# A decoder layer with routed experts: the lists of expert blocks in fewer VectorE operations

## The chip, the cores and the metric

The kernel runs on one core of one Trainium2 chip. The metric is the device time of one execution in microseconds (us); the time of a kernel is the median of its runs. TensorE is called PE here, VectorE DVE, ScalarE ACT, GpSimd POOL and SyncE SP, as in the profile.

## The reference

One decoder layer in float32, for 8 sequences of 112 tokens (896 rows of 512). Three sublayers, each followed by a sum with its input and a layernorm:

```python
x = _layernorm(x + attn(x, W_Q, W_K, W_V, W_O))              # 16 heads of 128, causal softmax
x = _layernorm(x + xattn(x, ctx_2048, Wq, Wg, bg, Wkv, Wo))  # linear attention over 375 rows, gated
x = _layernorm(x + ffn(x, router, gate_up, down))            # 8 experts of 512, two per token
```

The last one is what the change touches:

```python
logits = h @ router_weight.T + router_bias
top_vals, top_idx = jax.lax.top_k(logits, TOP_K)             # TOP_K = 2 of E = 8
top_w = jax.nn.softmax(top_vals, axis=-1)
scores = jnp.zeros_like(logits).at[jnp.arange(T)[:, None], top_idx].set(top_w)
gate_up = jnp.einsum('th,ehj->etj', h, gate_up_proj) + gate_up_proj_bias[:, None, :]
...
act = (up + 1.0) * (gate * jax.nn.sigmoid(gate * ALPHA))     # gate and up clipped at 7
expert_out = jnp.einsum('eti,eih->eth', act, down_proj) + down_proj_bias[:, None, :]
out = jnp.einsum('te,eth->th', scores, expert_out)
```

The kernel computes an expert only for the tokens routed to it.

## The kernel before, in words

**Stages.** The 896 rows are 7 tiles of 128. Self-attention runs first, head by head. Then cross-attention: for each sequence b the projections of its context (`project_pair`, matmuls L776), a summary of keys and values (`summarize`, L830), and the division and gating (`attend`, L858 to L870: a reciprocal L868 and the product L870 into `gate`). As soon as the rows of tile t are gated, the generator `close(t)` runs beside this work in small pieces, one piece at each `tick()`: the output projection (L261) and the sum (L268), the second layernorm (statistics L239 and L241 on DVE, square root L243 on ACT, L245 and L246 on DVE), and then the router `route(t)`.

**Router.** `route(t)` transposes the rows (L530, copied by ACT at L533), multiplies them with the router's weights (L537), picks the two best experts (L545 to L554), and counts with two matmuls (L562, L563) how many rows each expert has had. `upto[:, t, e]` starts at e * 896 (T is 896) and grows by tile: it is the next free row of expert e in a store in DRAM, where each expert owns 7 blocks of 128 rows. L587 scatters the rows there (two indirect DMAs from POOL).

**Lists.** The expert phase runs in 18 steps. Each handles 128 rows of one expert, or, in the 8 "paired" steps, twice 64 rows of one or two experts. Which expert and which block a step takes is not known until the router has counted, so `list_blocks(i)` computes it on DVE, at five points: after tiles 3, 4 and 5 for the steps 0, 1 to 2 and 3 to 4 (lists 0 to 2, only full blocks), and after the last tile for the last five steps (list 3) and the paired ones (list 4, in blocks of 64 rows). All of it is on tiny tiles: 8 experts, 1 to 8 steps, the same on every partition. For each list the kernel takes the count of an expert's rows, compares it with the block limits `blocks7` (L633) and sums the results (L618): the number of blocks. What earlier lists had (`taken`) is subtracted (`left`, L641), a running sum over experts follows (L646), which is compared with the step's own number in `place` (L650, `past`). The sum of `past` is the step's expert (`es`, as integer `eb[:, 0]`), and the sum of `past` times `jump` (L652 to L654) is the step's block (`eb[:, 1]`, L662). L682 to L686 work out how many blocks each expert got, for the next list. For the last list `changed` (L669) notes whether a step's expert differs from that of the step before in the same buffer, so that its weights need no new load.

**Who reads the lists.** SP reads `eb` into registers (L921) and issues the loads of the expert's weights (L952 `wg` and `wu`, L962 `wd`, 1 MB each, into `slab`), ACT does so for the biases (L987), POOL for the blocks of tokens (L1006). `start(s)` compares a token's first expert with `es` (L1054).

**Order.** The order of the instructions on PE, DVE, ACT and SP is the order in which the program issues them. It is fixed from the start of the loop over b. In this order a list stands on DVE just behind `route(t)` of its tile and ahead of what the loop does next: behind list 0 come the sum and the layernorm of tile 4; behind list 1 the key maps (L788 to L806) and the gating (L867 to L870); behind list 2 the spreading of step 0's biases (L995); behind lists 3 and 4 the spreading of step 2's biases, the sum of step 0's result (L1183), and the gate and up values of step 2 (L1151 to L1160), which PE transposes next (L1040, `aT_ps`). Each engine works its queue in that order, each instruction waiting for its own inputs.

**Expert steps.** In a step PE multiplies with `wg` and `wu` (L1143, `gups`), DVE adds the biases and makes the gated product, PE transposes it and multiplies with `wd` (L1172, `yps`). Twelve slabs hold the weights of four lanes; a lane's next weights are fetched when PE has read the old ones. Steps 5 to 12 are the paired ones; the fetch of step 5 is the first that needs list 4.

Of the kernel before, what the change touches and what calls it, by code (L numbers as in the profile page):

```python
# [10 lines left out]
F32 = mybir.dt.float32  # L11
# [3 lines left out]
ALU = mybir.AluOpType  # L15
AX = mybir.AxisListType
# [3 lines left out]
P = 128  # L20
B, S, D = 8, 112, 512
T = B * S
NT = T // P
# [6 lines left out]
E, I = 8, 512  # L30
W = 516
XF, XD, XS, XK = 512, 513, 514, 515
NB = T // P
NQ = 4
HB = P // 2
# [25 lines left out]
def decoder_layer(ctx: ExitStack, tc: tile.TileContext, t_in: dict, out: bass.AP):  # L61
    nc = tc.nc

    const = ctx.enter_context(tc.tile_pool(name="const", bufs=1))
# [38 lines left out]
    def counting(name: str, shape, pattern):  # L103
        c = const.tile(shape, F32, name=name)
        nc.gpsimd.iota(
            c,
            pattern=pattern,
            base=0,
            channel_multiplier=0,
            allow_small_or_imprecise_dtypes=True,  # L110
        )
        return c
# [5 lines left out]
        out=before,  # L118
# [7 lines left out]
    allones = const.tile([P, P], F32, name="allones")  # L126
    nc.vector.memset(allones, 1.0)
    expert = counting("expert", [P, E], [[1, E]])
    blocks7 = counting("blocks7", [P, E, NB], [[0, E], [P, NB]])

    place = []
    for i, (_, at) in enumerate(LISTS[:-1]):
        n = at.stop - at.start
# [20 lines left out]
    upto = counting("upto", [P, NT + 1, E], [[0, NT + 1], [T, E]])  # L154
# [443 lines left out]
    es = const.tile([P, STEPS], F32, name="es")  # L598
    eb = const.tile([P, 3, STEPS], I32, name="eb")

    taken = const.tile([P, len(LISTS) + 1, E + 1], F32, name="taken")
    nc.vector.memset(taken, 0.0)

    totals = {}

    def list_blocks(i: int):

        t, steps = LISTS[i]
        n = steps.stop - steps.start
# [7 lines left out]
        def summed(out, e_last):  # L617
            nc.vector.tensor_reduce(out, e_last, AX.X, ALU.add)  # L618
            return out

        def per_step(e_row):
            return e_row.unsqueeze(1).broadcast_to([P, n, E])

        left, upto_e, jump = each("left"), each("upto_e"), each("jump")
        if not last:
            count = each("count")
            nc.vector.tensor_sub(count, upto[:, t, :], upto[:, 0, :])  # L627
            several = (False, True) if t == NT else (True,)
            for over_half in several:
                cmp = const.tile([P, E, NB], F32, name=f"cmp_{i}_{over_half}")  # L630
                if t == NT and over_half:
                    nc.vector.tensor_scalar_add(count, count, -float(HB))
                nc.vector.tensor_tensor(  # L633
                    cmp,
                    count.unsqueeze(2).broadcast_to([P, E, NB]),
                    blocks7,
                    ALU.is_gt if t == NT else ALU.is_ge,
                )

                totals[over_half] = summed(each(f"total{over_half}"), cmp if t == NT else cmp[:, :, 1:])  # L640
            nc.vector.tensor_sub(left, totals[True], had[:, :E])  # L641
        else:
            nc.vector.tensor_scalar_mul(had, had, 2.0)
            nc.vector.tensor_add(left, totals[False], totals[True])
            nc.vector.tensor_sub(left, left, had[:, :E])
        nc.vector.tensor_tensor_scan(  # L646
            upto_e, allones[:, :E], left, 0.0, ALU.mult, ALU.add
        )
        past = const.tile([P, n, E], F32, name=f"past_{i}")
        nc.vector.tensor_tensor(past, per_step(upto_e), place[i], ALU.is_le)  # L650

        nc.vector.tensor_sub(jump, had[:, 1:], had[:, :E])  # L652
        nc.vector.tensor_sub(jump, jump, left)
        nc.vector.tensor_scalar_add(jump, jump, float(of_expert))  # L654
        summed(es[:, steps], past)
        nc.vector.tensor_scalar_min(es[:, steps], es[:, steps], float(E - 1))
        nc.vector.tensor_copy(eb[:, 0, steps], es[:, steps])
        nc.vector.tensor_mul(past, past, per_step(jump))
        blk = const.tile([P, n], F32, name=f"blk_{i}")
        summed(blk, past)  # L660
        nc.vector.tensor_add(blk, blk, place[i][:, :, 0])
        nc.vector.tensor_scalar(  # L662
            eb[:, 1, steps], blk, had[:, 0:1], float(E * of_expert), ALU.add, ALU.min
        )

        def changed(now, then, half=None):
            on = slice(0, P) if half is None else slice(half * HB, (half + 1) * HB)
            a, b = es[on, now], es[on, then]
            nc.vector.tensor_tensor(  # L669
                eb[on, 2, now], a, b.broadcast_to(a.shape), ALU.not_equal  # L670
            )
# [31 lines left out]
    with tc.tile_pool(name="cross", bufs=2) as cr:  # L703
# [213 lines left out]
        halves = store.rearrange("(n p) w -> n p w", p=HB)  # L917
# [168 lines left out]
        for b in range(B):  # L1086
# [6 lines left out]
            else:  # L1093
                work = iter(())
                steps = [start(0, side, "bT")]
# [24 lines left out]
    with tc.tile_pool(name="moe", bufs=2, reuse_waits="tile") as moe:  # L1120
# [182 lines left out]
        for s in range(STEPS + 1):  # L1303
# [53 lines left out]
            if before_:  # L1357
# [75 lines left out]
```

## Time and profile before

| what | value |
|---|---|
| time before | 978.79 us, median of 3 runs (977.5, 978.79, 979.02) |
| the profiled execution | 978.09 us, of which the span is 976.5 |
| PE busy | 920.5 us, 94% of the span, 3915 matmuls |
| DVE busy | 502.6 us, 51%, 1117 instructions |
| ACT busy, POOL busy | 247.3 us, 206.1 us |
| mean granted clock of PE | 0.98 |
| lists 0, 1, 2 on DVE | 675.77 to 679.48, 701.42 to 705.19, 736.49 to 740.29 |
| lists 3 and 4 on DVE | 759.65 to 767.74 |

The profile is one execution seen by the hardware profiler. Times count from the start of the span. A row of the timeline gives start, duration, engine, line, operation and output<-input; brackets at its end give the time that the engine was idle before it and what ended that. A row of waits gives the engine, the line that waited, the engine and line that released it, and then total, number and longest of the waits in us. In the view of stretches, each engine's busy us and instructions stand for a stretch of time, then the granted clock of PE (1.00 is full), the mean busy share of the DMA engines, and GB/s.

Lists 0 to 2 are 21 DVE instructions each, lists 3 and 4 together 39. Each takes 0.15 to 0.4 us, and many overlap with the one before.

### The profile page before, as it was taken

Reading aid. Unit: us, or ns where it says so; the run is one execution under the profiler, and the core shown is the slowest. Engines: PE = TensorE matmul, PEld = TensorE weight load, DVE = VectorE, ACT = ScalarE, POOL = GpSimd, SP = SyncE. Lnnn points to the kernel's source line nnn. Section 1 sums busy time; section 2 is a strip of 40 time slices with the busy share of each in tenths; the row PEclk is TensorE's granted clock in tenths of the full one; section 3 lists DMA queues with packets and bytes.
Section 4 is the critical chain, followed back from the end, with each engine's and each line's share of the span. In section 5 each row is a group of like instructions: output and inputs, shape, how many; then the busy total and the mean of one; then the engine's idle time right before and its main releaser. Section 6 shows DMA issues by size and latency. Waiting matters only on the chain. (4 is left out here: it accounts for less than half of the span.)

```text
span 976.5 us, 11044 instructions
## 1 busy us (share of the span) xinstructions
PE 920.5 (94%) x3915; PEld 467.9 (48%) x3915; DVE 502.6 (51%) x1117; ACT 247.3 (25%) x429; POOL 206.1 (21%) x267
## 2 busy tenths in 40 slices
PE   7998999999999999999999999997969999999981
PEld 3465644466445564664554445454544443334440
DVE  1356521145312552456430756677558864556785
ACT  1133311033102330332322233322224322222232
POOL 3133300021101230302002212212102332222343
PEclk9999999999999999999999999999979999999997
DMA  8995004102011001021100111112356899768953
GB/s 339 348 349 210 1 1 172 44 0 87 1 44 43 1 1 43 1 89 60 32 1 1 32 33 54 54 55 69 143 212 258 282 366 371 270 240 342 386 180 133
DMA packets 35063, 130.48 MB, mean 134 GB/s; under 512 B 3862, under 2 KB 8022, under 8 KB 25152
## 3 DMA queue, kind: packets, MB, share of 16 engines
q1 hardware_dynamic: 29296, 114.01, 32.0%
q0 software_dynamic: 4768, 14.98, 4.3%
q10 hardware_dynamic: 944, 0.79, 0.3%
q8 instruction: 31, 0.51, 0.2%
q14 instruction: 24, 0.20, 0.1%
HBM read 122.02 MB, written 30.06 MB: 156 GB/s over the span
## 5 line engine op out<-in xcount | busy, mean ns | idle before, releaser
L1143 PE MATMUL gups<-slab,bT 128*64 128x512 f32 (+1 forms) x416 | 134.1, 602 | 1.2 <-DMA slab<-in_wu_dram 1.2
L261 PE MATMUL ops<-slab,zT 128*128 128x512 f32 x224 | 97.9, 593 | 0.0
L1143 PEld LDWEIGHTS gups<-slab,bT 128*64 128x64 f32 (+1 forms) x416 | 49.1, 160 | 69.5 <-issue 67.4
L299 POOL TENSOR_TENSOR ws<-slab 128x256 f32<-128x256 f32 x16 | 11.6, 727 | 281.1 <-PE qk_5c L315 83.0
L1172 PE MATMUL yps<-slab,aT 128*64 128x512 f32 (+1 forms) x208 | 68.2, 601 | 0.9 <-ACT aT L1044 0.7
L261 PEld LDWEIGHTS ops<-slab,zT 128*128 128x128 f32 x224 | 42.0, 190 | 50.3 <-issue 49.5
L351 PE MATMUL vps<-slab,x0T 128*112 128x512 f32 x128 | 59.4, 619 | 1.0 <-DVE x0T L211 0.8
L1151 DVE TENSOR_TENSOR gu<-gups,biases 128x512 f32<-128x512 f32 x36 | 24.8, 689 | 59.5 <-PE gups L1143 59.5
L268 DVE TENSOR_TENSOR xn<-xn,ops 128x512 f32<-128x512 f32 x28 | 19.2, 685 | 55.3 <-PE ops L261 55.2
L1044 ACT COPY aT<-aT_ps 128x512 f32<-128x512 f32 x18 | 10.5, 585 | 133.5 <-PE aT_ps L1040 133.4
L1172 PEld LDWEIGHTS yps<-slab,aT 128*64 128x64 f32 (+1 forms) x208 | 24.8, 160 | 37.7 <-issue 35.2
L466 DVE COPY zT<-zps 128x448 f32<-128x448 f32 x32 | 20.0, 624 | 39.8 <-PE zps L459 39.8
L459 PEld LDWEIGHTS zps<-pT,v 112*128 112x128 f32 x256 | 33.5, 192 | 12.3 <-issue 11.2
L351 PEld LDWEIGHTS vps<-slab,x0T 128*112 128x112 f32 x128 | 23.0, 185 | 31.7 <-issue 30.0
L435 DVE TENSOR_REDUCE nm<-p 112x4 f32<-112x448 f32 x32 | 19.7, 615 | 30.5 <-POOL p L425 30.5
L261 PE MATMUL xops<-slab,gate 128*128 128x512 f32 x56 | 27.4, 635 | 7.1 <-DVE gate L870 7.1
L459 PE MATMUL zps<-pT,v 112*128 112x112 f32 x256 | 33.4, 273 | 0.0
L587 POOL DMA_INDIRECT store<-xn,rows x14 | 14.0, 1000 | 82.5 <-DVE count L627 58.8
L1185 POOL DMA_INDIRECT parts<-y,nums x16 | 16.9, 1056 | 62.6 <-DVE y L1183 48.6
L995 DVE STREAM_SHUFFLE biases<-biases 128x1024 f32<-128x1024 f32 (+1 forms) x28 | 30.0, 1104 | 0.0
L419 ACT ACTIVATE p<-sps 112x448 f32<-112x448 f32 x32 | 17.4, 543 | 45.6 <-PE sps L411 45.6
L411 PE MATMUL sps<-k,q 128*112 128x112 f32 x256 | 28.0, 262 | 0.0
(816 smaller groups left out, 1676.6 us busy)
## 6 DMA issues: line engine op xcount, KB each, us to landing
slab<-in_wg_dram SPq DMA_DIRECT2D x26, 1024.0 KB
slab<-in_wu_dram SPq DMA_DIRECT2D x26, 1024.0 KB
slab<-in_wd_dram SPq DMA_DIRECT2D x26, 1024.0 KB
store<-slab SPq DMA_DIRECT2D x8, 1806.0 KB
cT<-in_ctxT_dram SPq DMA_DIRECT2D x8, 750.0 KB
slab<-in_wq_dram SPq DMA_DIRECT2D x4, 1024.0 KB
slab<-in_wk_dram SPq DMA_DIRECT2D x4, 1024.0 KB
slab<-in_wo_dram SPq DMA_DIRECT2D x4, 1024.0 KB
```

The costliest lines, as they stand in the source:

```text
L261: nc.tensor.matmul(ps, aT[:, c, t * P : (t + 1) * P], w[:, c, :], start=(c == 0), stop=(c == C - 1),)
L268: nc.vector.tensor_add(xn[:, t, :], xn[:, t, :], ps)
L351: nc.tensor.matmul(ps[:S, :], xT[:, c, b * S : (b + 1) * S], w[:, c, :], start=(c == 0), stop=(c == C - 1),)
L411: nc.tensor.matmul(ps[:S, i * S : (i + 1) * S], qk["q"][:, rows], qk["k"][:, rows], start=True, stop=True,)
L419: nc.scalar.activation(p.rearrange("s b m -> s (b m)"), ps[:S, :HALF], AF.Copy, scale=1.0 / math.sqrt(DH),)
L435: nc.vector.tensor_reduce(nm, p, AX.X, ALU.max, negate=True)
L459: nc.tensor.matmul(zps[:, i * S : (i + 1) * S], v[:, half * 4 + i, hl * DH : (hl + 1) * DH], pT[:, i * S : (i + 1) * S], start=True, stop= ...
L466: nc.vector.tensor_copy(zT[:, hl, half * HALF : (half + 1) * HALF], zps[:, :HALF])
L995: nc.vector.stream_shuffle(b, b, [0] * XH)
L1143: nc.tensor.matmul(ps[rows_], st["bT"][:, c, rows_], slab[3 * q + k][:, c, :], start=(c == 0), stop=(c == C - 1),)
L1151: nc.vector.tensor_add(a, ps, st["bias"][:, k * I : (k + 1) * I])
L1172: nc.tensor.matmul(ps[rows_], st["aT"][:, c, rows_], slab[3 * q + 2][:, c, :], start=(c == 0), stop=(c == C - 1 and s < STEPS - 1),)
```

## The change

`list_blocks` computes the same lists with fewer operations, and three constants or tiles change with it. On DVE a list of the first three has 13 instructions instead of 21, and the last two together have 24 instead of 39. The order on PE, ACT, POOL and SP stays.

- The constant `blocks7` (8 x 7) becomes `first_rows` (8 x 14): for each expert the first rows of its half blocks, e * 896 + 64 k. `upto` is compared with it directly, so the count is no longer worked out; full blocks are every second entry. With all tiles in, one comparison with all 14 gives both sums: of the odd entries for list 3, of all for list 4.
- `jump` is made in one operation, for 7 experts instead of 8, from `taken` and the total. `past` has 7 experts too, so that the expert's number can't pass 7 and the clamp goes.
- The product of `past` and `jump` is written into `place`, whose eighth entry still holds the step's number: the sum over it gives the block without another addition.
- The running sum is written behind a zero (`ends_`), so that it can be read shifted by one. What each expert got comes from it in two operations instead of five. The zeros need five small memsets at the start.

```diff
-    blocks7 = counting("blocks7", [P, E, NB], [[0, E], [P, NB]])
+    first_rows = counting("first_rows", [P, E, 2 * NB], [[T, E], [HB, 2 * NB]])
...
+    jumps = [const.tile([P, E], F32, name=f"jump_{i}") for i in range(len(LISTS))]
+    ends_ = [const.tile([P, E + 1], F32, name=f"ends_{i}") for i in range(len(LISTS))]
+    for x in ends_:
+        nc.vector.memset(x[:, 0:1], 0.0)
...
-            count = each("count")
-            nc.vector.tensor_sub(count, upto[:, t, :], upto[:, 0, :])
-            several = (False, True) if t == NT else (True,)
-            for over_half in several:
-                cmp = const.tile([P, E, NB], F32, name=f"cmp_{i}_{over_half}")
-                if t == NT and over_half:
-                    nc.vector.tensor_scalar_add(count, count, -float(HB))
-                nc.vector.tensor_tensor(
-                    cmp,
-                    count.unsqueeze(2).broadcast_to([P, E, NB]),
-                    blocks7,
-                    ALU.is_gt if t == NT else ALU.is_ge,
-                )
-                totals[over_half] = summed(each(f"total{over_half}"), cmp if t == NT else cmp[:, :, 1:])
-            nc.vector.tensor_sub(left, totals[True], had[:, :E])
+            begun = first_rows if t == NT else first_rows[:, :, 2::2]
+            cmp = const.tile([P, *begun.shape[1:]], F32, name=f"cmp_{i}")
+            nc.vector.tensor_tensor(
+                cmp,
+                upto[:, t, :].unsqueeze(2).broadcast_to(begun.shape),
+                begun,
+                ALU.is_gt if t == NT else ALU.is_ge,
+            )
+            total = each("total")
+            nc.vector.tensor_reduce(total, cmp[:, :, 1::2] if t == NT else cmp, AX.X, ALU.add)
+            if t == NT:
+                totals["halves"] = each("halves")
+                nc.vector.tensor_reduce(totals["halves"], cmp, AX.X, ALU.add)
         else:
             nc.vector.tensor_scalar_mul(had, had, 2.0)
-            nc.vector.tensor_add(left, totals[False], totals[True])
-            nc.vector.tensor_sub(left, left, had[:, :E])
+            total = totals["halves"]
+        left = each("left")
+        nc.vector.tensor_sub(left, total, had[:, :E])
+        nc.vector.scalar_tensor_tensor(
+            jumps[i][:, : E - 1], had[:, 1:E], float(of_expert), total[:, : E - 1], ALU.add, ALU.subtract
+        )
         nc.vector.tensor_tensor_scan(
-            upto_e, allones[:, :E], left, 0.0, ALU.mult, ALU.add
+            ends_[i][:, 1:], allones[:, :E], left, 0.0, ALU.mult, ALU.add
         )
         past = const.tile([P, n, E], F32, name=f"past_{i}")
-        nc.vector.tensor_tensor(past, per_step(upto_e), place[i], ALU.is_le)
-        nc.vector.tensor_sub(jump, had[:, 1:], had[:, :E])
-        nc.vector.tensor_sub(jump, jump, left)
-        nc.vector.tensor_scalar_add(jump, jump, float(of_expert))
-        summed(es[:, steps], past)
-        nc.vector.tensor_scalar_min(es[:, steps], es[:, steps], float(E - 1))
+        nc.vector.tensor_tensor(
+            past[:, :, : E - 1], per_step(ends_[i][:, 1:E]), place[i][:, :, : E - 1], ALU.is_le
+        )
+        nc.vector.tensor_reduce(es[:, steps], past[:, :, : E - 1], AX.X, ALU.add)
+        nc.vector.tensor_mul(place[i][:, :, : E - 1], past[:, :, : E - 1], per_step(jumps[i][:, : E - 1]))
         nc.vector.tensor_copy(eb[:, 0, steps], es[:, steps])
-        nc.vector.tensor_mul(past, past, per_step(jump))
         blk = const.tile([P, n], F32, name=f"blk_{i}")
-        summed(blk, past)
-        nc.vector.tensor_add(blk, blk, place[i][:, :, 0])
+        nc.vector.tensor_reduce(blk, place[i], AX.X, ALU.add)
+        if not last:
+            got = each("got")
+            nc.vector.scalar_tensor_tensor(
+                got, ends_[i][:, :E], float(n), had[:, :E], ALU.min, ALU.subtract
+            )
         nc.vector.tensor_scalar(
             eb[:, 1, steps], blk, had[:, 0:1], float(E * of_expert), ALU.add, ALU.min
         )
+        if not last:
+            nc.vector.scalar_tensor_tensor(
+                taken[:, i + 1, :E], ends_[i][:, 1:], float(n), got, ALU.min, ALU.subtract
+            )
...
-        else:
-            got = each("got")
-            nc.vector.tensor_sub(got, upto_e, left)
-            nc.vector.tensor_scalar(got, got, -1.0, float(n), ALU.mult, ALU.add)
-            nc.vector.tensor_scalar_max(got, got, 0.0)
-            nc.vector.tensor_tensor(got, got, left, ALU.min)
-            nc.vector.tensor_add(taken[:, i + 1, :E], got, had[:, :E])
```

More of the change, by code (lines that the diff above doesn't have):

```diff
@@ L615, in each @@
             return const.tile([P, E], F32, name=f"{name}_{i}")
-        def summed(out, e_last):
-            nc.vector.tensor_reduce(out, e_last, AX.X, ALU.add)
-            return out
         def per_step(e_row):
-            return e_row.unsqueeze(1).broadcast_to([P, n, E])
-        left, upto_e, jump = each("left"), each("upto_e"), each("jump")
+            return e_row.unsqueeze(1).broadcast_to([P, n, e_row.shape[1]])
         if not last:
-            count = each("count")
-            nc.vector.tensor_sub(count, upto[:, t, :], upto[:, 0, :])
-            several = (False, True) if t == NT else (True,)
-            for over_half in several:
-                cmp = const.tile([P, E, NB], F32, name=f"cmp_{i}_{over_half}")
-                if t == NT and over_half:
-                    nc.vector.tensor_scalar_add(count, count, -float(HB))
-                nc.vector.tensor_tensor(
-                    cmp,
-                    count.unsqueeze(2).broadcast_to([P, E, NB]),
-                    blocks7,
-                    ALU.is_gt if t == NT else ALU.is_ge,
-                )
-                totals[over_half] = summed(each(f"total{over_half}"), cmp if t == NT else cmp[:, :, 1:])
-            nc.vector.tensor_sub(left, totals[True], had[:, :E])
```

## The prediction

> **What bounds the kernel now.** I read the page first, then the waits of PE (TensorE) after 600 us, the timeline around each of the five lists, and the stretches of the granted clock.
>
> ```profile
> PE   7998999999999999999999999997969999999981
> DVE  1356521145312552456430756677558864556785
> PEclk9999999999999999999999999999979999999997
> ```
>
> PE is full in nearly every slice, so only a stretch where it stalls can pay. The dents lie in slices 28 to 30 (about 683 to 757 us), where VectorE (DVE) is busy and builds the lists; the clock dips there too. The waits of PE in 600 to 976 us give the names:
>
> ```profile
> PE xops L261 <- DVE gate L870: 5.9, 4, 3.2
> PE kvps_10a L776 <- ACT biases L797: 3.9, 1, 3.9
> PE aT_ps L1040 <- DVE gu L1160: 1.2, 1, 1.2
> PE gups L1143 <- DMA slab<-in_wu_dram: 1.2, 1, 1.2
> ```
>
> List 0 in the timeline (start, duration, engine, line; idle time before in brackets):
>
> ```profile
> 675.77 0.16 DVE L627 TENSOR_TENSOR count<-upto 128x8 f32<-128x8 f32 x1
> 675.97 0.22 DVE L633 TENSOR_TENSOR cmp_True<-count,blocks 128x56 f32<-128x56 f32 x1
> ...
> 676.87 0.17 DVE L650 TENSOR_TENSOR past<-upto_e,place 128x8 f32<-128x8 f32 x1
> 676.96 0.16 DVE L652 TENSOR_TENSOR jump<-taken 128x8 f32<-128x8 f32 x1
> 677.15 0.17 DVE L653 TENSOR_TENSOR jump<-jump,left 128x8 f32<-128x8 f32 x1
> ...
> 679.48 0.68 DVE L268 TENSOR_TENSOR xn<-xn,xops 128x512 f32<-128x512 f32 x1
> 681.13 0.29 ACT L243 ACTIVATE sd_ln<-mv_ln,eps 128x1 f32<-128x1 f32 x1 [4.75 <-DVE mv_ln L241]
> 681.34 0.57 ACT L797 COPY biases<-kvps_10a 125x512 f32<-125x512 f32 x1
> 682.05 3.65 PE L776 MATMUL kvps_10a<-slab,biases 128*125 128x512 f32 x4 [3.94 <-ACT biases L797]
> ```
>
> The waits blame ACT, but ACT's copy L797 queues behind L243, L243 behind the layernorm statistics on DVE, and these behind the list. So all of it is on PE's path. The four matmuls after the stall took 3.65 us; the same four at 687.68 take 1.88. Stretches of 3.4 us (columns: PE, PE loads, DVE, ACT, POOL busy, then PEclk, DMA share) show why:
>
> ```profile
> 678.70:682.10 3.40, 0.05 (x1) 0.09 (x1) 2.80 (x10) 0.77 (x2) 0.59 (x1) 1.00 0.88 268
> 682.10:685.50 3.40, 3.40 (x4) 1.36 (x5) 0.70 (x2) 0.00 (x0) 0.00 (x0) 0.50 0.97 395
> 709.40:712.80 3.40, 0.19 (x2) 0.18 (x2) 3.26 (x4) 0.58 (x1) 0.00 (x0) 1.00 0.99 409
> 712.80:716.20 3.40, 3.40 (x5) 1.34 (x6) 2.02 (x4) 1.91 (x2) 0.00 (x0) 0.50 1.04 428
> 716.20:719.60 3.40, 2.25 (x9) 1.01 (x7) 1.48 (x3) 0.00 (x0) 0.00 (x0) 1.00 1.01 419
> 719.60:723.00 3.40, 1.59 (x100) 1.34 (x100) 1.64 (x8) 0.77 (x2) 0.00 (x0) 1.00 0.20 77
> ```
>
> After an idle stretch the next one runs at half clock. A stall near 3.4 us is thus paid about one and a half times.
>
> **What the change does to a list.** Lists 0, 1, 2 go from 21 DVE instructions to 13, lists 3 and 4 together from 39 to 24. Instruction order on every other engine is unchanged. In list 0 an operation that needs the one before it starts 0.20 us after it (L652 to L653: 0.19), one that doesn't starts 0.08 to 0.09 after it (L650 to L652). Laying the 13 new ones on these steps: compare to total 0.25, total to left 0.24 (both as now), left to ends 0.20 with jump in between, ends to past 0.21, past to the expert sum 0.20, to the product 0.08, product to the block sum 0.20 with the copy in between, to the block number 0.19 with got in between, to taken 0.13, to the next operation 0.09: 1.79 us, against 679.48 - 675.77 = 3.71 now.
>
> - **List 0:** 1.92 us less. The path behind it (L268, statistics, L243, L797, 2.57 us to the matmul) keeps its length, so the stall falls from 3.94 to 2.02; the layernorm is what is late next. At full clock the four matmuls take 1.88: another 1.77. Together 3.69.
> - **List 1** (701.42 to 705.19, 3.77): after it DVE runs without a gap through L868 (reciprocal, 2.95) to the gate L870, for which PE waits 3.21. By the same steps it saves 1.94; the stall falls to 1.27, held by the reciprocal. The eight matmuls behind it took 5.37 at half clock against 3.65 normal: 1.72. Together 3.66.
> - **List 2** (736.49 to 740.29): saves 1.95 on DVE, but PE waits only 0.79 after it (x2T at 746.05 for DVE). Gain 0.79; the rest is slack, for from 746.05 to 773.7 PE doesn't wait.
> - **Lists 3 and 4** (759.65 to 767.74, 8.09): the same steps with a compare of 112 elements (0.31) and rows of 35 to 56 elements (0.21 to 0.27 a step) give 2.14 + 2.32, the six comparisons at the end (0.67) included: 4.46, so 3.6 less. PE waited 1.22 for L1160, and waits no more: 1.22; PE is the bound next.
>
> The end of the last two lists also starts transfers:
>
> ```profile
> 767.07 0.74 DVE L669 TENSOR_TENSOR eb<-es 64x2 int32<-64x2 f32 x6
> 768.63 1.02 SPq L952 DMA_DIRECT2D slab<-in_wg_dram  x2
> ...
> 774.98 0.63 PE L1040 MATMUL aT_ps<-ident,gu 128*128 128x128 f32 x4 [1.22 <-DVE gu L1160]
> ...
> 824.34 3.22 PE L1143 MATMUL gups<-slab,bT 128*64 128x512 f32 x13 [1.21 <-DMA slab<-in_wu_dram]
> ```
>
> From 764 to 768 us the DMA share is 0.33 and from 772 to 840 it is 1.0: that stretch starts when SP reads the list. It starts 3.6 earlier relative to PE's own start, PE comes 1.22 earlier, so the transfers win 2.4, and the DMA waits at 824.34 (1.21) and 840.58 (0.21) go: 1.42. The slack left at 840 is 3.6 - 1.22 - 1.42 = 1.0 us. Everything else in this phase (POOL's token fetches, ACT's bias fetches) is started by PE's or DVE's progress and moves along.
>
> **Costs of the edit.** Five memsets (0.06 each, as L101) run before 2.5 us, where DVE then idles 4.39 us for PE's first result: nothing, at most 0.3 without that cover. The larger count table on POOL (0.32 now, at most doubled) is done before 5.2 us, while POOL idles until 17.6: nothing, at most 0.3. Fused operations: no such row of 8 elements with a constant; its bounds are L1067 (0.15) and L1058 (0.22), I take 0.17 as L683. Reading every second word in compare and sum has no row. Below it is bounded by zero, since the same elements read densely are the rows I used. Above, the Trainium skill (Vector Engine (DVE) Microarchitecture Reference, 5.2 Measured stream behaviour) puts lone-word steps at up to 2.5 ns an element against 1.05: 48 elements, an estimate of 0.07 us in a list and 0.2 for all the stalls that count. It speaks against the change; I take zero, since the 0.20 steps are mostly fixed cost.
>
> The same section gives about 75 ns per instruction once the queue overlaps. By that, 8 fewer operations save 0.6 a list and 15 fewer save 1.1, the stalls stay long enough to halve the clock, and the gain is 3 x 0.6 + 1.1 = 2.9 us. The row says 0.20 a step, because nearly every removed operation waits for the one before it. I go by the row.
>
> For the clock, the Trainium skill (TensorE: Matmul & The Clock Gate, Part 1: The HAM clock gate) has free-running windows of 3.4 us, an idle one giving half rate, and its table warns only of gaps above some 3 us. By that, stalls of 2.0 and 1.3 cost no clock: 3.5 us gained. The trace is stricter: after a window with 1.59 us of PE work the clock halved, after 2.25 it did not. The stalls left allow windows with 1.4 to 2.1 us of work, in between. I take no halving, since the 1.59 was mostly small matmuls; the other end gives 3.5 back.
>
> **Sum.** 3.69 + 3.66 + 0.79 + 1.22 + 1.42 = 10.8. The profiled execution took 978.09 (span 976.5, 1.6 around it): 967.3. The median of the runs, 978.79, lies 0.7 above it: 968.0.
>
> **Rivals.**
> - *One or both clock halvings stay:* 969.8 to 971.5. For it the 1.59 row; against it, dense matmuls. 25%.
> - *The transfers don't start earlier* (SP or a buffer of an expert's weights still in use holds them: the last such buffer is read until 766.9): the 1.42 and the 1.22 come back as DMA waits, 970.6. Against it: two megabytes into free buffers go first. 9%.
> - *The list isn't what PE waits for* (the page's small rules: 75 ns an operation): 975.9. 6%.
> - *Within 0.2%:* the time is pinned by the saturated transfers up to 840, 978. Against it: they idle before 768 and are started by DVE. 3%.
> - *Slower:* the half-clock stretch of 723 to 736.7 us, four windows where small matmuls and waits on ACT alternate, lasts longer as it starts in another phase of the window. Each further window costs 1.7 us; seven or more in a row, 24 us, are needed to eat 10.8 (985 at ten). Nothing shows such a stretch: dense matmuls ended it after one window. 3%.
> - *As forecast,* 966.5 to 969.5: 54%.
>
> The range, 964.0 to 972.5, takes in the clock's ends and one window less in the half-clock stretch (966.3), but not the last three rivals. Over 0.2% (2 us, about what measurement can tell from no change): faster 0.94, same 0.03, slower 0.03.
>
> **What would show it.** List 0 at 1.8 us with 0.08 and 0.20 steps; a stall of 2.0 before kvps_10a and 1.3 before xops, with full clock after both; no wait of aT_ps for L1160; the fetch of two wg at least 3 us earlier than PE's shift; no DMA wait at the later gups. Steps longer than 0.25 in the new operations, or PE idle at 824 or 840, would prove me wrong.

## The result, and the profile after

The changed kernel takes 967.6 us (median of 4 runs, 966.68 to 969.56). Beside it the kernel before took 978.9 (4 runs, 977.5 to 981.18): a ratio of 0.9893, interval [0.9873, 0.9912]. The forecast was 968.0. The profiled execution after took 968.43 us, of which the span is 966.6.

The busy tenths and the granted clock, as before in 40 slices:

```profile
PE   7998999999999999999999999999969999999981
DVE  1356521145312643357440667677668755555895
PEclk9999999999999999999999999999979999999996
```

The slices alone hardly show it: one dent of PE and one of the clock are still there. The waits of PE in 600 to 976 us (total, number, longest):

```profile
PE xops L262 <- DVE gate L874: 4.1, 4, 1.4
PE lps L538 <- ACT x2T L534: 3.4, 1, 3.4
PE x2T_ps L531 <- DVE is_first L1058: 2.5, 1, 2.5
PE kvps_10a L780 <- ACT biases L801: 2.0, 1, 2.0
PE aT_ps L1044 <- DVE gu L1164: 0.9, 1, 0.9
PE bT_ps L1044 <- DMA xblk<-store: 0.6, 1, 0.6
```

The stall behind list 0 went from 3.9 to 2.0, the longest at xops from 3.2 to 1.4, and no wait for `gups` on a DMA is left. The `aT_ps` row is not that of before: it lies in the last expert steps, not behind the lists. New is a wait of 0.6 for a block of tokens. List 0 in the timeline, with what stands behind it:

```profile
675.23 0.20 DVE L630 TENSOR_TENSOR cmp<-upto,first_rows 128x48 f32<-128x48 f32 x1
675.47 0.20 DVE L637 TENSOR_REDUCE total<-cmp 128x8 f32<-128x48 f32 x1
675.71 0.17 DVE L645 TENSOR_TENSOR left<-total,taken 128x8 f32<-128x8 f32 x1
675.79 0.16 DVE L647 SCALAR_TENSOR_TENSOR jump<-taken,total 128x7 f32<-128x7 f32 x1
675.91 0.18 DVE L650 TENSOR_TENSOR_SCAN ends<-allones,left 128x8 f32<-128x8 f32 x1
...
676.92 0.18 DVE L672 SCALAR_TENSOR_TENSOR taken<-ends,got 128x8 f32<-128x8 f32 x1
677.02 0.68 DVE L269 TENSOR_TENSOR xn<-xn,xops 128x512 f32<-128x512 f32 x1
```

From 675.23 to 677.02 is 1.79 us. L650 needs `left` (L645) and starts 0.20 after it; `jump` (L647), which doesn't, starts 0.08 after L645. And PE behind the two lists, and where the last two lists end:

```profile
679.58 1.95 PE L780 MATMUL kvps_10a<-slab,biases 128*125 128x512 f32 x4 [2.02 <-ACT biases L801]
706.56 3.67 PE L262 MATMUL xops<-slab,gate 128*128 128x512 f32 x8 [1.43 <-DVE gate L874]
764.77 0.60 PE L1044 MATMUL aT_ps<-ident,gu 128*128 128x128 f32 x4
765.92 0.63 PE L1044 MATMUL bT_ps<-ident,xblk 128*128 128x128 f32 x4 [0.55 <-DMA xblk<-store]
```

The first fetch of weights that needs list 4, and the fetch of the block of tokens that PE waits for at 765.92:

```profile
756.59 1.02 SPq L956 DMA_DIRECT2D slab<-in_wg_dram  x2
757.59 0.57 POOL L1010 DMA_DIRECT2D xblk<-store  x1 [4.13 <-DMA store<-xn,rows]
```

The four matmuls take 1.95 where they took 3.65, and the eight 3.67 where they took 5.37: full clock. In stretches of 3.4 us:

```profile
676.20:679.60 3.40, 1.38 (x5) 0.34 (x3) 2.90 (x13) 0.77 (x2) 1.35 (x2) 1.00 0.56 111
679.60:683.00 3.40, 3.40 (x8) 1.51 (x9) 0.74 (x2) 1.41 (x2) 0.00 (x0) 1.00 0.90 360
703.20:706.60 3.40, 1.97 (x6) 0.63 (x4) 3.26 (x4) 0.59 (x1) 0.00 (x0) 1.00 1.01 420
706.60:710.00 3.40, 3.40 (x8) 1.51 (x9) 2.13 (x4) 1.87 (x2) 1.14 (x2) 1.00 1.02 426
```

PE did 1.38 us of work in a stretch of 3.4 and kept its clock (column behind POOL).

How far PE is ahead of the kernel before, taken from the starts of the same matmuls in the two profiled executions:

| at | before, us | after, us | ahead by | step |
|---|---|---|---|---|
| kvps_10a, ahead of the stall | 674.51 | 673.97 | 0.54 | 0.54 |
| kvps_10a, behind the stall | 682.05 | 679.58 | 2.47 | +1.93 |
| kvps_10c | 685.53 | 681.37 | 4.16 | +1.69 |
| xops behind list 1 | 712.65 | 706.56 | 6.09 | +1.93 |
| bT_ps behind it | 717.85 | 710.07 | 7.78 | +1.69 |
| x2T_ps behind list 2 | 746.05 | 737.26 | 8.79 | +1.01 |
| aT_ps behind lists 3 and 4 | 774.98 | 764.77 | 10.21 | +1.42 |
| bT_ps behind it | 775.44 | 765.92 | 9.52 | -0.69 |
| aT_ps of a later step | 834.84 | 823.46 | 11.38 | +1.86 |
| aT_ps of a later step | 859.08 | 847.33 | 11.75 | +0.37 |
| last aT_ps | 951.07 | 940.77 | 10.30 | -1.45 |

The first 0.54 was there ahead of the first list, so it is the difference of two executions and not the change. Without it the sum is 11.2 at 859 us and 9.8 at the last `aT_ps`. The profiled executions lie 9.7 apart with it and 9.1 without; the medians lie 11.3 apart.

### The profile page after: what moved, and what is told of

Read it like the earlier page. It is cut to its first block, busy times and chain, and to the rows that moved or that the text cites. A ratio compares the mean times of both kernels' runs of the same rounds, so it can differ in the third digit from the quotient of the medians.

```text
span 966.6 us, 11011 instructions
## 1 busy us (share of the span) xinstructions
PE 915.7 (95%) x3915; PEld 467.8 (48%) x3915; DVE 498.8 (52%) x1083; ACT 247.6 (26%) x429; POOL 206.9 (21%) x267
## 4 chain that ended last, share of the span: by engine, by line
PE 80%; DVE 12%; issue 3%; ACT 2%; DMA 1%; POOL 1%; ACTq 0%; POOLq 0%; DVEq 0%
PE gups L1147 11%; PE ops L262 10%; PE vps L352 6%; PE yps L1176 4%; PE zps L460 3%; PE xqps L899 2%; PE xgps L899 2%; PE sps L412 2%; PE xops L262 2%; DVE z L872 2%; PE pps L452 1%; DMA xblk<-store 1%; DVE p L437 1%; PE sumps L834 1%; PE kvps_11a L780 1%
## 5 line engine op out<-in xcount | busy, mean ns | idle before, releaser
L300 POOL TENSOR_TENSOR ws<-slab 128x256 f32<-128x256 f32 x16 | 11.6, 727 | 281.3 <-PE qk_5c L316 83.0
```

## The experiments

Theory: what counts is the length of a list on VectorE, 0.20 us for each small step that waits for the one before; the stalls behind lists 0 and 1 shrink one for one, the clock's loss behind them goes, and the last two lists start transfers earlier. Rivals: small operations cost 0.08 whatever feeds them; the clock stays lost; the transfers set the end anyway. All kernels below were measured over 5 rounds, those of one group on one chip beside the kernel before (medians 978.2, 978.6 and 978.9 in the three groups).

### Which lists carry the gain

Kernels with the new form for some of the lists only (the old function is kept beside the new one, with its temporaries shared between lists to make room), and the changed kernel again. The lists in `OLD` keep the old form; the edit shown is that for list 0 alone.

```
+OLD = (1, 2, 3, 4)
...
 def list_blocks(i):
+    if i in OLD:
+        return list_blocks_old(i)
```

**Only list 0:** 

> Only list 0 in the new form, lists 1 to 4 as before (their temporary tiles shared, to make room). Theory: the stall of PE ahead of the second pair of kvps_10a falls from 3.94 to 2.0 us, the four matmuls behind it take 1.9 instead of 3.65, so that kvps_10c starts 3.7 us earlier counted from the start of the first kvps_10a; the waits of list 1 (3.2), list 2 (0.8), aT_ps (1.2) and of the DMA (1.4) stay. Time 3.7 below before. Rival (a fixed 75 ns an operation): the stall falls by 0.6 only and the clock still halves, 0.6 below before. Rival on the clock: the stall falls but the clock halves all the same, 1.9 below before.

**Lists 0 to 2:** 

> Lists 0 to 2 in the new form, 3 and 4 as before (temporary tiles shared). Theory: 3.7 + 3.7 + 0.8 = 8.1 us below before; the wait of aT_ps (1.2) and the DMA waits at the later gups and yps (1.4) stay as in before. Rival (the saturated transfers up to 840 us pin the time): PE comes 8 us earlier at the later gups and waits there that much longer, so within 1 us of before.

**Lists 3 and 4:** 

> Lists 3 and 4 in the new form, 0 to 2 as before (temporary tiles shared). Theory: the stalls at kvps_10a (3.9) and xops (3.2) with their half clock stay, the wait of aT_ps for the gated product is gone (1.2) and so are the DMA waits behind it (1.4), since the fetch of step 5 starts 3.6 us earlier: 2.6 us below before. Rival (transfers don't start earlier): the DMA waits stay or grow and take the 1.2 back, 0 to 1.2 below before.

**The changed kernel again:** 

> The changed kernel once more, unaltered, for a second profile and more runs. Theory: 10.8 us below before, PE ahead of before's by 11 to 12 us at 890 us in the trace; the 1.8 us that the first profile lost behind 928 us belongs to that execution and is seen in a different size. Rival: the tail loses the same 1.8 us every time, since it is held by something that doesn't move with PE (the loads of the results, or VectorE's own work).

**Lists 1 and 2**, in a later group: 

> Only lists 1 and 2 in the new form; lists 0, 3 and 4 as before. The sum of the prediction's steps for these two is 3.66 + 0.79 = 4.5 us below before, 973.8 us. Theory (the gains add): what lists 0, 1 and 2 gave together less what list 0 gave alone is 7.4 us, so 970.9 us. Rival (list 0's gain, and the clock behind it, came only with the other two): about 4.5 us or less below before, 973.8 us or more.

| new form for | median, us | ratio to before, interval | below before by | forecast's steps |
|---|---|---|---|---|
| list 0 | 976.25 | 0.9977 [0.9968, 0.9987] | 2.0 | 3.7 |
| lists 1 and 2 | 973.43 | 0.9939 [0.992, 0.9957] | 5.5 | 4.45 |
| lists 0, 1 and 2 | 968.88 | 0.9901 [0.9885, 0.9917] | 9.4 | 8.1 |
| lists 3 and 4 | 975.87 | 0.9978 [0.9968, 0.9988] | 2.4 | 2.6 |
| all | 967.5 | 0.9889 [0.9872, 0.9906] | 10.7 | 10.8 |

Lists 0 to 2 bring most of the whole (9.4 of 10.7), so the end is not pinned by the transfers; lists 3 and 4 bring what was worked out for them. The parts add up (2.0 + 5.5 + 2.4 = 9.9 against 10.7, with about 1 to 2 us of uncertainty on each). List 0 alone is a miss: 3.7 lies outside its interval (1.3 to 3.1 us). But its median stands where few of its 22 runs do: nine took 973.8 to 975.3 us, about 3.9 below before (median 974.4), ten took 977.3 to 978.9, about 0.3 below, and three lie between. The profiled execution (978.12) is one of the slower ones, so what follows is of these at most; of the quicker ones, which fit the forecast's 3.7, there is no profile. Its timeline shows the stall as forecast, and the clock lost all the same:

```profile
679.03 2.48 PE L873 MATMUL kvps_10a<-slab,biases 128*125 128x512 f32 x4 [2.01 <-ACT biases L894]
...
743.00 1.08 PE L533 MATMUL x2T_ps<-ident,xn 128*128 128x128 f32 x4 [3.51 <-DVE is_first L1151]
743.88 5.95 PE L1240 MATMUL gups<-slab,bT 128*128 128x512 f32 x8
```

The same stall of 2.01 was followed by half clock here, for 3.4 us. And what PE had gained by 732 us (2.75 more, with 10.2 us of half clock from 717 us on instead of 13.6) it lost at 743: it came to `x2T_ps` before the old list 2 was done and waited 3.51 (0.79 before). The eight `gups` behind that took 5.95 at half clock, where eight at 735.89 took 3.60. By 774.67 nothing of the gain was left in this execution. So list 2 can be worth more when the lists before it are short. For lists 1 and 2 that makes 7.4 (9.4 - 2.0) possible; 5.5 was measured, with an interval of some 4.2 to 7.8 that holds 4.5 and 7.4 alike. How much of each list's gain depends on the others stays open within that.

The changed kernel's second profiled execution took 971.29 us, the longest of its six runs. Counted from ahead of the lists, PE was 11.6 us ahead of before at 850 us (11.2 in the first), as expected. The loss in the tail was expected in a different size and came in the same one, which is what the rival said: from that `aT_ps` (847.33 in the first, 850.17 in the second, 859.08 before) to the end of the span the two executions took 119.3 and 119.2 us, before took 117.4.

### What a small operation costs, and how long a stall costs the clock

Eight, or twice four, subtractions of 128 x 8 whose result nobody uses, in front of list 0 (and list 1):

```
+EXTRA = {0: 8}                                   # {0: 4, 1: 4} for twice four
...
+            if i in EXTRA:
+                spare = const.tile([P, E], F32, name=f"spare_{i}")
+                nc.vector.tensor_sub(spare, upto[:, t, :], upto[:, 0, :])
+                for _ in range(EXTRA[i] - 1):    # dependent: each reads the one before
+                    nc.vector.tensor_sub(spare, spare, upto[:, 0, :])
```

In the independent form each of the eight writes its own tile from `upto`. In that kernel and in the one with twice four, lists 0 to 2 also share one `cmp` tile, to make room.

**Eight dependent:** 

> The changed kernel with eight further VectorE subtractions of 128 x 8 in front of list 0, each fed by the one before it; nothing uses their result. Theory (a dependent small step costs 0.20 us and the stall at kvps_10a follows list 0 one for one, with the half clock coming back behind a stall of about 4 us): list 0's place on VectorE grows by 1.6 us, the stall at kvps_10a from 2.02 to about 3.6 us, the clock halves behind it in the profiled execution, and the time rises by 1.6 us (clock kept) to 3.4 us (clock lost): 969.2 to 971 us. Rival (every VectorE instruction costs the same whether it is fed by the last or not, some 0.075 us): stall 2.6 us, time up by 0.6 us. Rival (a later transfer sets the end anyway): stall 3.6 us and time unchanged.

**Eight independent:** 

> The changed kernel with eight further VectorE subtractions of 128 x 8 in front of list 0, none of which reads what another one writes. Theory (an independent small step costs 0.08 us, a dependent one 0.20): they take 0.65 us of VectorE's time where the eight dependent ones took 1.5, the stall at kvps_10a is about 2.7 us, and the time rises by 0.6 us if the clock stays full behind it, by about 2.4 if a stall of that length already halves it: 968 to 970. Rival (small operations cost the same, fed by the last or not): stall 3.5 us as with the dependent ones.

**Four dependent at each of lists 0 and 1:** 

> The changed kernel with four dependent subtractions of 128 x 8 in front of list 0 and four in front of list 1, half the dose at two places. Theory (0.20 us each): stalls of 2.8 us at kvps_10a and 2.2 us at xops, and the time up by 1.6 us if the clock stays full behind both, by up to 5 if it halves behind both. What it tells: whether the clock's loss sets in between a stall of 2.0 and one of 2.8 us, or only near 3.5.

The rows of the added operations and of the first one of list 0 behind them, in the kernel with eight dependent ones and then in that with eight independent ones:

```profile
674.89 0.16 DVE L631 TENSOR_TENSOR spare<-upto 128x8 f32<-128x8 f32 x1
675.08 1.37 DVE L633 TENSOR_TENSOR spare<-spare,upto 128x8 f32<-128x8 f32 x7
676.37 0.20 DVE L636 TENSOR_TENSOR cmp<-upto,first_rows 128x48 f32<-128x48 f32 x1
```

```profile
675.36 0.72 DVE L633 TENSOR_TENSOR spare<-upto 128x8 f32<-128x8 f32 x8
676.01 0.20 DVE L637 TENSOR_TENSOR cmp<-upto,first_rows 128x48 f32<-128x48 f32 x1
```

Eight dependent ones move the list by 1.48 us (0.19 each), eight independent ones by 0.65 (0.08 each). The stall at kvps_10a grew by the same: 3.46 and 2.64 against 2.02. That answers the first rival. The times: 970.5 (ratio 0.9912 [0.9894, 0.993]), 968.54 (0.9891 [0.9868, 0.9913]) and 970.82 (0.9917 [0.9898, 0.9937]); beside 967.5 these are 3.0, 1.0 and 3.3 more, or 2.6, 0.4 and 2.6 if each is counted from the kernel before of its own group. The intervals of the outer two overlap a little with that of the changed kernel, that of the middle one almost wholly; what tells them apart is the profile.

The clock shows in one number for each execution. It runs from the first kvps_10a to kvps_11a, less the stall in between, which is always the same work.

| kernel | stall at kvps_10a | first kvps_10a to kvps_11a, less the stall | clock |
|---|---|---|---|
| before | 3.94 | 15.19 | halved |
| lists 3 and 4 only | 3.92 | 14.96 | halved |
| lists 1 and 2 only | 3.94 | 15.19 | halved |
| eight dependent | 3.46 | 15.19 | halved |
| four dependent, twice | 2.68 | 15.19 | halved |
| eight independent | 2.64 | 15.19 | halved |
| list 0 only | 2.01 | 15.19 | halved |
| after; lists 0 to 2; after again; bias fetches moved | 2.02; 2.01; 2.01; 2.01 | 13.50 | full |

The clock's loss is 1.69 us in six of the seven, 1.46 in the other. Behind a stall of 2.6 or more it came in all six executions, behind 2.0 in one of five; these are single profiled executions, each of another kernel but for two of the changed one. At xops, where half clock had followed a stall of 3.2, it never followed one of 1.4, nor one of 2.06 (the kernel with four and four). So the forecast's full clock held behind xops in each of these, and behind kvps_10a in four of five. With 0.6 us more in list 0 it was lost in both executions seen; for the eight independent ones that makes 0.62 of stall and 1.69 of clock, while their median rose by 0.4 to 1.0 only, so how often it is lost there stays open. The kernel with four and four:

```profile
676.30:679.70 3.40, 0.78 (x2) 0.00 (x0) 2.89 (x13) 0.77 (x2) 0.96 (x1) 1.00 0.73 220
679.70:683.10 3.40, 3.35 (x6) 1.38 (x7) 0.81 (x2) 0.64 (x2) 0.59 (x1) 0.67 1.00 359
683.10:686.50 3.40, 3.40 (x11) 1.76 (x10) 1.02 (x2) 1.45 (x2) 0.00 (x0) 0.83 1.00 421
705.70:709.10 3.40, 1.34 (x5) 0.30 (x3) 3.26 (x4) 0.59 (x1) 0.47 (x1) 1.00 0.95 397
709.10:712.50 3.40, 3.40 (x8) 1.51 (x9) 2.13 (x4) 1.87 (x2) 0.00 (x0) 1.00 1.03 429
```

In the kernel with four and four, 0.78 us of work in 3.4 was followed by half clock (0.67 and 0.83 on average over a boundary that lies in between), 1.34 was not. But list 0 alone, with 1.39 us of work in the stretch from 676.2 to 679.6, lost it, and after, with 1.38 in the same stretch, kept it: neither the stall nor the work in a stretch laid so decides alone. What does isn't shown.

### What is still waited for

If the stalls left are the lists themselves, standing ahead of what PE needs, they can be moved behind it. And the 3.4 us at `lps` come from ACT, which issues four bias fetches (L991) ahead of the copy of x2T (L534); the last of them and the copy, after:

```profile
716.92 0.52 ACTq L991 DMA_DIRECT2D biases<-in_db_dram  x1
717.48 0.59 ACT L534 COPY x2T<-x2T_ps 128x512 f32<-128x512 f32 x1 [4.78 <-DMA biases<-in_db_dram]
```

```
                 if t == n - 1:
+                    for _ in range((2, 2, 0, 0, 0)[i]):
+                        yield
                     list_blocks(i)
...
-                fetch_biases(0)
-                fetch_biases(1)
                 fetch_down(1)
                 fetch_inner(2)
             next(work, None)
             tick()
             sums = summarize(b)
             tick()
+            if b == B - 1:
+                fetch_biases(0)
+                fetch_biases(1)
```

**Lists moved (first edit):** 

> The changed kernel with lists 0 and 1 moved behind work that TensorE waits for: list 0 behind the layer norm, the feature and the copy that stand after it on VectorE, list 1 behind the gate's reciprocal and product. Nothing else changes place. Theory (the two stalls left, 2.02 us at kvps_10a and 1.43 us at xops, are the lists themselves, standing ahead of what TensorE needs): the stall at kvps_10a falls to 0.2 to 0.5 us and that at xops to 0 to 0.2, and the time falls by about 3 us below the changed kernel, to some 964.5 us. Rival (the lists are needed early for the fetches of the token blocks, so that moving them delays landings): TensorE's wait for the token block ahead of bT_ps grows from 0.55 to over 1.5 us and the time stays within 1 us of the changed kernel's. Rival (lists 0 and 1 only hid other steps of VectorE's or ScalarE's that then come last): the stalls keep more than 1.2 us each.

**Bias fetches moved (second edit):** 

> The changed kernel with the two fetches of biases that ScalarE issues moved behind the next tick of the last sequence, so that ScalarE copies x2T ahead of them. VectorE's order is untouched. Theory (the 13.6 us of half clock behind 715 us come from the wait of 3.4 us for the copy of x2T, which stands behind the fetches on ScalarE): the wait at lps falls under 1 us, less of the stretch runs at half clock, and the time falls by 2 to 6 us. Rival (the next step to be late is VectorE's is_first, for which the router waits): the wait moves to x2T_ps with 1.5 us or more and the half clock stays, time within 1 us of the changed kernel's. Rival (the fetches land later and the first steps of the experts wait for their biases): slower by 1 us or more.

**Both:** 

> The changed kernel with both moves: lists 0 and 1 further back on VectorE, and the two fetches of biases further back on ScalarE. Theory: the two gains add, about 3 us from the lists and what the other run shows for the fetches, 959 to 964 us. Rival (both gains are of the same half clock): no more than the larger of the two alone.

**Both, and list 1 further** (five yields, and the fetches that read list 1 behind the second tick): 

> The kernel with both moves, with list 1 moved once more, from behind the gate to behind the layer norm of the last tile and the four small steps after it; the fetches that read list 1 move behind it. Theory (the 3.4 us that TensorE waits for x2T_ps there hold list 1's 1.8 us): that wait falls to 1.6 us, and the time by 1.8 us more, to about 960.7 us. Rival (the weights of step 1 are fetched about 6 us later, and TensorE waits for them at the first gups of that step): a DMA wait of over 1 us at gups, time unchanged or worse than the kernel with both moves.

| kernel | median, us | ratio to before, interval | below before by |
|---|---|---|---|
| changed kernel again | 967.5 | 0.9889 [0.9872, 0.9906] | 10.7 |
| lists moved | 965.95 | 0.9864 [0.9845, 0.9884] | 12.7 |
| bias fetches moved | 964.01 | 0.985 [0.9826, 0.9873] | 14.6 |
| both | 962.51 | 0.9832 [0.9813, 0.9851] | 16.1 |
| both, list 1 further | 963.61 | 0.9834 [0.9812, 0.9857] | 15.3 |

PE's rows in the kernel with the lists moved:

```profile
681.28 1.95 PE L780 MATMUL kvps_10a<-slab,biases 128*125 128x512 f32 x4 [0.24 <-ACT biases L801]
707.51 3.67 PE L262 MATMUL xops<-slab,gate 128*128 128x512 f32 x8 [0.68 <-DVE cmp L630]
714.99 0.63 PE L531 MATMUL x2T_ps<-ident,xn 128*128 128x128 f32 x4 [3.38 <-DVE is_first L1060]
```

The stall at kvps_10a fell by 1.78, the list's length, to 0.24: the list was nearly all of it. At xops 0.68 stayed, not 0 to 0.2. There the row names the list's `cmp`, but the gate's product (L874) ends at 707.36, just ahead of PE's start, so it is the gate that is left. The wait at `x2T_ps` grew from 2.49 to 3.38; list 1 now stands ahead of that tile's layer norm. PE's wait for the block of tokens is 0.78, not the 1.5 of the rival. The gain over the changed kernel, 2.0 us counted from before, is less than the 3 expected, and the two intervals overlap.

With the bias fetches moved the wait at `lps` is gone, and with it, in the profiled execution, the half clock of 715 to 728.6 us. First after, then the kernel with the fetches moved:

```profile
715.00:718.40 3.40, 0.28 (x2) 0.28 (x2) 1.07 (x2) 0.90 (x2) 0.00 (x0) 0.52 0.38 148
718.40:721.80 3.40, 3.40 (x17) 3.40 (x18) 1.20 (x7) 0.97 (x1) 0.00 (x0) 0.50 0.02 5
721.80:725.20 3.40, 3.40 (x15) 2.88 (x15) 3.25 (x2) 0.00 (x0) 0.00 (x0) 0.50 0.00 0
725.20:728.60 3.40, 3.40 (x6) 1.33 (x5) 2.89 (x15) 0.75 (x2) 0.00 (x0) 0.50 0.00 0
```

```profile
711.60:715.00 3.40, 1.26 (x84) 1.12 (x88) 1.98 (x8) 1.35 (x3) 0.00 (x0) 1.00 1.00 412
715.00:718.40 3.40, 3.08 (x61) 2.97 (x50) 2.85 (x10) 0.00 (x0) 0.00 (x0) 1.00 0.46 187
718.40:721.80 3.40, 2.89 (x11) 1.60 (x11) 3.26 (x3) 1.28 (x1) 0.00 (x0) 1.00 0.04 7
```

In its profile PE is 7.6 us further ahead of after by the next xops, counted from ahead of the lists; the 3.4 of the wait are in that. On the way to the end PE waits 1.74 at the next `x2T_ps` (not at all after) and 2.44 for a block of tokens (0.55 after), with 3.4 us of half clock behind the latter, and the profiled executions end 5.7 apart. The six runs fall into two groups: three took 961.1 to 962.8 us with a mean granted clock of 0.990 to 0.992, three took 965.3 to 966.8 with 0.981 to 0.982, like the changed kernel (0.980 to 0.985). The profiled execution is of the first group. The 13.6 us of half clock make an estimated 0.007 of the mean clock (half of 13.6 in 961), a little less than the step between the groups. So the half clock seems to come back, there or elsewhere, in half of the executions, and the median, 964.01, lies where no run does.

Both moves together give 962.51, some 5 us below the changed kernel; there the intervals of the ratios lie apart. Counted from before, the two gains (2.0 and 3.9) come to 5.9 and both together to 5.4; in the profile of both, a wait of 3.38 at `x2T_ps` came with 10.2 us of half clock. The interval overlaps with that of the bias fetches alone, so the rival, no more than the larger of the two, isn't excluded. List 1 moved once more brought nothing that shows: the wait at `x2T_ps` fell to 2.49, not to 1.6, and a block of tokens came late:

```profile
764.88 0.84 PE L1046 MATMUL bT_ps<-ident,xblk 128*128 128x128 f32 x4 [3.54 <-DMA xblk<-store]
```

It is the rival's kind of loss, at another transfer than the one it named: tokens, not weights. But this is the block of the fifth step, whose place is in list 2. The two blocks that list 1 places were used at 727.83 and 738.38 without a wait, and the kernel with only the bias fetches moved, where list 1 stands in its old place, waits 2.44 at the same point. POOL issued the fetch of this block at 755.87, 6.4 us after its issue of the scatter of the last rows; with both moves alone these were 752.66 and 4.3. That moving list 1 made it late isn't shown.

## Why the prediction held, step by step

- **The length of a list.** List 0 was put at 1.79 us and took 1.79; list 1 took 1.84, list 2 1.82, lists 3 and 4 together 4.42 against 4.46. Reading every second word cost nothing visible: the compare of 48 elements, which reads its constant so, took 0.20 us, against 0.22 for the old one of 56, and list 3's sum over every second word (56 of them) took 0.21. The choice of 0.20 and 0.08 by dependence is what the added subtractions measured. The section "5.2 Measured stream behaviour" of the Trainium skill's Vector Engine (DVE) Microarchitecture Reference, with its 75 ns, fits the independent ones only (0.08 here); the dependent ones take 0.19.
- **Stalls behind lists 0 and 1.** Forecast 2.02 and 1.27, measured 2.02 and 1.43; PE gained 1.93 at each (1.92 and 1.94 forecast). The move of list 0 shows that the list was all but 0.24 of the stall left there; at xops the gate itself holds 0.68 of the 1.43.
- **Clock.** Forecast 1.77 and 1.72, measured 1.69 twice. The choice of no halving was right in both profiled executions of the changed kernel, but it was closer than "dense matmuls" said: behind the same stall of 2.0 the clock went in one execution of list 0 alone, and behind 2.64 and 2.68 it went in the one execution seen of each. That it held is partly luck: what decides at a stall of 2.0 isn't known, and the rival given 25% came in a near relative of this kernel. The rule of the Trainium skill that the prediction weighed (TensorE: Matmul & The Clock Gate; the table is in the section Why this matters for your kernels) warns of gaps above some 3 us: here stalls of 2.64 and 2.68 were followed by half clock.
- **List 2.** 0.79 forecast, 1.01 measured.
- **Lists 3 and 4.** The wait of 1.22 at `aT_ps` went, as forecast. Not foreseen was what came next: a block of tokens that had been covered by that wait, and took 0.69 back at 766. Its fetches (POOL, L1010) follow the scatter of the rows, not the list. It was said that they "move along"; they did, but PE came sooner.
- **Transfers.** The first fetch of `wg` that needs list 4 went from 768.63 to 756.59, 12.0 earlier, where PE was 8.8 ahead: 3.2 (3.6 forecast, at least 3 asked for). PE's waits for weights at `gups` and `yps` (1.42) are gone, and PE gained 2.2 between the `bT_ps` of 766 and the `aT_ps` of 847 us: these 1.42 and the 0.69 lent before. The kernel with only lists 3 and 4 gives the same from the other side, 2.4 against 2.6 (one wait of 0.36 at `yps` was left there).
- **What the sum left out.** Up to 859 us of before the gain is 11.2 against 10.8. By the end 1.85 of it was gone in the profiled execution, and 1.81 in the second one: a VectorE addition of 128 x 512 (L1241) took 2.18 and 2.19 us where it took 0.69 before, and PE waited for VectorE (0.91 us at the `aT_ps` of 940.77). Before and after, with the addition that POOL makes near it:

```profile
937.36 0.69 DVE L1237 TENSOR_TENSOR xn<-xn,seconds 128x512 f32<-128x512 f32 x1
938.32 1.27 POOL L1205 TENSOR_TENSOR y<-y,biases 128x512 f32<-128x512 f32 x1
```

```profile
925.97 2.18 DVE L1241 TENSOR_TENSOR xn<-xn,seconds 128x512 f32<-128x512 f32 x1
926.32 1.27 POOL L1209 TENSOR_TENSOR y<-y,biases 128x512 f32<-128x512 f32 x1
```

After, POOL's addition falls into VectorE's; before, it begins behind it. The tail of four profiled executions in which it falls so (the two of the changed kernel, eight independent, lists 1 and 2 only) took 118.5 to 119.3 us, that of the ten others 116.6 to 117.9. So the loss goes with the overlap; the sum has no term for it. The medians, 10.7 to 11.3 apart, tell neither how often it happens nor what it costs them.
- **A slip in the reading.** A slice of the page is 24.4 us long, so slices 28 to 30 are 659 to 732 us, not 683 to 757; no term of the sum rests on it.

So the forecast was right in its mechanism and nearly in each size up to 859 us. That 968.0 and 967.6 lie 0.4 us apart is luck: the difference is below what separates two groups of runs, and the sum lacks both the 0.4 to 0.8 that PE gained beyond it up to 859 us and the 1.8 lost in the tail. Between medians, undoing lists 0 to 2 leaves 2.4, undoing lists 3 and 4 leaves 9.4, and lengthening list 0 by 1.5 us costs 2.6 to 3.0, where the profile shows 1.44 of stall and 1.69 of clock.

## What to carry to other kernels

Count small VectorE operations by their chain: here one that needs the last cost 0.19 to 0.20 us, one that doesn't cost 0.08, and it matters only where an engine that sets the end waits behind the chain. Shortening a stall of TensorE by a microsecond or two can pay double if it takes the stall out of the range where the clock halves, and whoever shortens it should ask what stood hidden behind it: here a copy on ScalarE, a layer norm, a block of tokens. Moving the chain behind what TensorE needs takes away a stall as well as shortening it does, until something else comes last: here the gate at xops, and a block of tokens. And where the runs of a kernel fall into two groups, as with list 0 alone and with the bias fetches moved, a profile is of one of them: the median may lie where no run does.

## What the runs showed of the hardware that was not expected

- The half clock comes in pieces of about 3.4 us or multiples (6.8, 10.2, 13.6), and not in the same places in each execution. In six of fourteen profiled executions, of kernels that are alike up to there, PE ran at half clock for 3.4 or 6.8 us near 91 us. The three with 6.8 stood 2.7 to 2.9 us behind the kernel before, ahead of the first list, where those without such a piece up to there stood at most 0.1 behind and up to 1.1 ahead. That alone is a quarter of the gain studied here, and the reason why profiled executions are compared by intervals within them.
- The cost of one such piece behind kvps_10a, where PE works without a break, is 1.69 us, half of 3.4, for stalls from 2.01 to 3.94 (1.46 in one execution).
- The four additions of L1241 in the last expert steps (and their like in the other kernels) have one shape and take 0.67 to 0.71 us in 48 of the 56 rows of the fourteen profiled executions. In four executions the second of them took 1.26 to 1.28, in four others the third took 2.07 to 2.19. In each of these eight an addition of POOL's overlaps with VectorE's, which ended 0.55 to 0.57 us behind it; with none of the 48 short ones does one overlap. So VectorE's addition is held up by POOL's, whichever of the two rows begins first. Not every VectorE operation is: the comparison L1271 of the kernel before (938.90, 0.66 us) runs inside POOL's addition of 938.32 to 939.59.
